# Attention values with a 37-column stationary operand, and its accumulator read by VectorE in two parts

## The chip, the cores and the metric

The kernel runs on one core of one Trainium2 chip. The metric is the device time of one execution in microseconds, the median of the runs shown. Lower is better. The engines are called TensorE (PE in the profile, PEld for its weight loads), VectorE (DVE), ScalarE (ACT), GpSimd (POOL) and SyncE (SP, which issues transfers).

## The reference

One block of a conditioned transformer, all in fp32: x is 2 x 2048 x 576, 16 heads of 36 features, a hidden layer of 2304.

```python
mod = silu(c) @ w_ada + b_ada                      # six vectors per batch: shifts, scales, gates
xn = layernorm(x) * (1 + sc_msa) + sh_msa
q, k, v = split(xn @ w_qkv + b_qkv)                # 16 heads of 36
q, k = layernorm(q, qn_g, qn_b), layernorm(k, kn_g, kn_b)
attn = softmax(einsum('bqhd,bkhd->bhqk', q, k) * 36 ** -0.5)
o = einsum('bhqk,bkhd->bqhd', attn, v)
x = x + g_msa * (o @ w_proj + b_proj)
xn2 = layernorm(x) * (1 + sc_mlp) + sh_mlp
x = x + g_mlp * (gelu(xn2 @ w1 + b1) @ w2 + b2)
```

## The kernel before

Each of the two batches goes through its queries, keys and values, then attention (`attend`, called once per batch), then the projection of the output; the hidden layer for both batches comes last. The change is in `attend`.

Attention works on pairs of heads (8), blocks of 512 queries (4) and groups of 4 x 128 keys (4): 128 steps per batch. A step has three parts.

- `scores` (L1536) makes scores transposed, with keys on partitions. Each of its two half steps fills four PSUM banks of 128 x 512, one for each of the four groups of 32 rows of TensorE's array, which work side by side. A bank gets two products: 32 of a head's 36 features (`qm`, `km`), then the other 4 in three parts (`qe`, `ke`). ScalarE takes the exponential of each bank (L1540) into a tile `pt` in SBUF, of which there are five.
- `values` (L1549) multiplies the step's eight exponentials with the values and adds them up in one bank, the accumulator: head 0 of the pair in its rows 0 to 63, head 1 in rows 64 to 127. The stationary operand is 64 columns of `vt` from the head's first one. A head has 37 columns there (`HV`): its 36 values and a column of ones, whose product is the softmax's denominator. The other 27 columns belong to the next head; the rows of the accumulator that they make are not used.
- VectorE reads the accumulator, all 128 rows at once, into an SBUF tile `ot`: copied in the first key group (L1603), added in the other three (L1605).

After the fourth group `finish` sends the two rows of denominators (row 36 of either half) to DRAM and back on 64 partitions each, and VectorE divides: a reciprocal of `den` (L1570) and a product over all 128 rows of `ot` (L1571). These are put into a list of later work and come some steps behind.

The eight banks of PSUM are one ring (`bank()`, a pool of eight buffers). A step takes nine: eight for scores and one for the accumulator. TensorE's and VectorE's instructions stand in the order in which the code is written. The loop issues the scores of a step first, and then the values of the step before it. The accumulator's bank comes up again eight banks later, as the last of the eight that the next step's scores fill: the fourth of its second half.

Two steps of the loop carry other work in hooks (L178 is the product of the conditioning weights). For the last accumulator of a batch `ot` is the spare tile `spare[9]`.

Of the kernel before, what the change touches and what calls it, by code (L numbers as in the profile page):

```python
# [8 lines left out]
F32 = mybir.dt.float32  # L9
# [3 lines left out]
ALU = mybir.AluOpType  # L13
# [3 lines left out]
P = 128  # L17
# [14 lines left out]
def dit_block(  # L32
# [25 lines left out]
    nc = tc.nc  # L58
# [7 lines left out]
    BLK = 512  # L66
    NBLK = N // BLK
    TPB = BLK // P
    NF = MLP // P
    HV = HD + 1  # L70
# [23 lines left out]
    def bank():  # L94

        return psum["b"].tile([P, 512], F32, tag="b", name="b") if "b" in psum else s_tile()[:, 0, :]
# [650 lines left out]
    def head_rows(first, count=HD):  # L747

        at = first
        while at < first + count:  # L750
            n = min(P - at % P, first + count - at)
            yield at // P, at % P, at - first, n
            at += n

    def block_of_small():
# [11 lines left out]
        held, spare = {}, []  # L767
# [10 lines left out]
        vt = kv.tile([P, NT * H * HV + 64 - HV], F32, name="vt")  # L778
# [85 lines left out]
        def take_k(p):  # L864
            m, e = km[p % 2], ke[p % 2]
            if p > 2:
                not_sooner(m)
                not_sooner(e)
            src = lambda c: slice(c * N // 2, (c + 1) * N // 2)
            rows_taken(nc.gpsimd, m, e, range(2), C + p * 2 * HD, src, slice(0, N // 2))  # L870
            full = slice(0, P)
            return [
                lambda: scaled(m, m, full, 1),
                lambda: parted(e[:, 0:BLK], full, 1),
                lambda: parted(e[:, BLK:], full, 1),
            ]
# [13 lines left out]
        def take_q(p, qb):  # L890
            i, full = qb % 2, slice(0, P)
            src = lambda c: slice(qb * BLK, (qb + 1) * BLK)
            rows_taken(nc.sync, qm[i], qe[i], range(2), p * 2 * HD, src, slice(0, BLK))
            return [lambda: scaled(qm[i], qm[i], full, 0), lambda: parted(qe[i], full, 0)]
# [623 lines left out]
        def attend(b, pool, hooks, key_rows):  # L1518

            def scores(p, qb, g):
                i, j = p % 2, qb % 2
                pts = []
                for k0 in (2 * g * P, (2 * g + 1) * P):
                    keys = slice(k0, k0 + P)
                    banks = [bank() for _ in range(4)]
                    for k, q, first in (  # L1530
                        (km[i], qm[j], True),
                        (ke[i].bitcast(F32R), qe[j].bitcast(F32R), False),
                    ):
                        for r0, ps in zip(range(0, P, 32), banks):
                            r = slice(r0, r0 + (DIMS if first else 4 * (HD - DIMS)))
                            nc.tensor.matmul(ps, k[r, keys], q[r, :], start=first, stop=not first)  # L1536
                    for c in range(2):
                        pt = pool.tile([P, 2, BLK], F32, name="pt", bufs=5)
                        for h in range(2):
                            nc.scalar.activation(pt[:, h, :], banks[2 * c + h], AF.Exp, scale=SCALE)  # L1540
                        pts.append((pt, k0 // P + c * NT // 2))
                return pts

            def values(p, pts):
                acc = bank()
                for pt, kc in pts:
                    for h in range(2):
                        v0 = (kc * H + 2 * p + h) * HV
                        nc.tensor.matmul(  # L1549
                            acc[64 * h : 64 * h + 64, :],  # L1550
                            vt[:, v0 : v0 + 64],
                            pt[:, h, :],
                            start=pt is pts[0][0],
                            stop=pt is pts[-1][0],
                        )
                return acc

            def finish(p, qb, ot, den=None):


                if den is None:
                    den = pool.tile([P, BLK], F32, name="den")
                for h in range(2):
                    sums = den_dram[b, p, qb, h, :]
                    nc.sync.dma_start(out=sums.unsqueeze(0), in_=ot[64 * h + HD : 64 * h + HD + 1, :])
                    nc.sync.dma_start(out=den[64 * h : 64 * h + 64, :], in_=sums.partition_broadcast(64))

                def divided(c0=0, c1=BLK):
                    part = slice(c0, c1)
                    nc.vector.reciprocal(den[:, part], den[:, part])  # L1570
                    nc.vector.tensor_tensor(ot[:, part], ot[:, part], den[:, part], ALU.mult)  # L1571
                    cols = slice(qb * BLK + c0, qb * BLK + c1)
                    for h in range(2):
                        for c, row, d, n in head_rows((2 * p + h) * HD):
                            for r in (row,) if c < FULL else (row, row + 64):
                                nc.sync.dma_start(
                                    out=held["qo"][r : r + n, c, cols], in_=ot[64 * h + d : 64 * h + d + n, part]
                                )

                return divided  # L1580

            steps = [(p, qb, g) for p in range(NPAIR) for qb in range(NBLK) for g in range(NG)]


            behind, later = None, [[] for _ in range(13)]
            ended = None
            for p, qb, g in [*steps, (None, None, None)]:
                pts = None if p is None else scores(p, qb, g)
                if (p, qb) == (0, 0) and g < len(key_rows):
                    key_rows[g]()  # L1590
                if g == 0 and (p, qb) != (NPAIR - 1, NBLK - 1):
                    for i, do in enumerate(take_q(*((p, qb + 1) if qb + 1 < NBLK else (p + 1, 0)))):
                        later[1 + i].append(do)
                if g == 1 and qb == 0 and p + 1 < NPAIR:
                    for i, do in enumerate(take_k(p + 1)):
                        later[3 + NG * i].append(do)
                if behind is not None:
                    bp, bqb, bg, bpts = behind
                    acc = values(bp, bpts)
                    if bg == 0:  # L1600
                        last = (bp, bqb) == (NPAIR - 1, NBLK - 1)
                        ot = spare[9][:, :BLK] if last else pool.tile([P, BLK], F32, name="ot", bufs=2)
                        nc.vector.tensor_copy(ot, acc)  # L1603
                    else:
                        nc.vector.tensor_tensor(ot, acc, ot, ALU.add)  # L1605
                    if p is None:
                        ended = finish(bp, bqb, ot, spare[10][:, :BLK])
                    elif bg == NG - 1:
                        later[2 if bp == NPAIR - 1 else 3].append(finish(bp, bqb, ot))
                if (p, qb, g) in hooks:  # L1610
                    due = hooks[p, qb, g]() or []
                    later[1] = due[:1] + later[1]
                    later[2] = due[1:] + later[2]
                later.append([])
                for do in later.pop(0):
                    do()
                behind = (p, qb, g, pts)
            for do in [do for group in later for do in group]:
                do()
            return ended  # L1620
# [411 lines left out]
        for j in range(TPB + 1):  # L2032
            n, i = divmod(j, TPB)
# [346 lines left out]
        def combined_blocks(out_m, outs):  # L2380

            one = hs.tile([P, QUARTER], F32, name="one", bufs=2)
            nc.scalar.copy(one, out_m[1])  # L2383
            r = hs.tile([P, 2, HALF], F32, name="r", bufs=9)
            left, right = r[:, :, 0:QUARTER], r[:, :, QUARTER:HALF]
            both = lambda ap: ap.unsqueeze(1).to_broadcast([P, 2, QUARTER])
            tt = nc.vector.tensor_tensor
            tt(left, outs[2, 6], both(one), ALU.add)
            tt(right, outs[5, 7], both(left[:, 1]), ALU.add)
            tt(left[:, 1], right[:, 1], out_m[4], ALU.subtract)  # L2390
            tt(right[:, 1], right[:, 1], out_m[5], ALU.add)
            tt(right[:, 0], right[:, 0], out_m[3], ALU.add)
            return r
# [57 lines left out]
        for i, (n, m) in enumerate(products):  # L2451
# [16 lines left out]
            r = combined_blocks(out_m, outs)  # L2468
# [67 lines left out]
```

## Time and profile before

| what | us |
|---|---|
| median of 3 runs | 3060.53 (3060.13 to 3061.5) |
| span of the profiled execution | 3061.8 |
| TensorE busy in it | 3039.6 |
| VectorE busy | 1706.3 |
| ScalarE busy | 1493.3 |
| GpSimd busy | 1000.6 |
| products of the values, L1549 | 935.0 busy, 4096 |
| reads of the accumulator into `ot`, L1603 and L1605 | 42.9 and 128.6 busy, 62 and 186 |

The profiled execution has no other time of its own than its span, from the first to the last instruction. The granted TensorE clock was 0.999 in it. An fp32 product shows as two records, so the 4096 records of L1549 are 2048 products. A row of a timeline gives the start in us from the span's start, the length in us, the engine and line, the operation, the tile written and those read, and how many records are merged; in brackets, for how long the engine had been idle and what ended that. A row of the groups gives busy time and mean ns of one, then the idle time ahead of it. A row of one line's instructions gives shortest, middle and longest ns.

### The profile page before, as it was taken

To read this page: it belongs to the slowest core of one execution; us is meant where nothing else is said; L and a number is where in the kernel's file an instruction comes from. 1 tells how busy PE (TensorE), PEld (TensorE's weight loads), DVE (VectorE), ACT (ScalarE), POOL (GpSimd) and SP (SyncE) were. 2 spreads that over 40 slices of the span, in tenths; PEclk is the share of its full clock that TensorE was granted. 3 is DMA by queue.
4 is the path that set the end of the run, shared out by engine and by line. 5 is a ranking of instruction groups with operands and counts; after the bars stand their busy time and mean duration, and the time that the engine had idled before them with its cause. 6 is when DMAs were issued, how large, how long until landed. Compare 5 with 4: busy or idle time off the path is not lost.

```text
span 3061.8 us, 51356 instructions
## 1 busy us (share of the span) xinstructions
PE 3039.6 (99%) x19015; PEld 1892.7 (62%) x19015; DVE 1706.3 (56%) x2644; ACT 1493.3 (49%) x2917; POOL 1000.6 (33%) x1263
## 2 busy tenths in 40 slices
PE   8999999999999999999999999999999999999998
PEld 6884333333333688633333333347888888999998
DVE  6773455445553666544434444447666664667666
ACT  2326666666666233466666666643555553000000
POOL 4551100132322445201101111115445544545543
PEclk9999999999999999999999999999999999999999
DMA  5773322333333454412222222236888887855554
GB/s 150 187 147 92 103 69 70 81 92 93 94 87 94 162 129 83 94 46 64 52 55 74 62 67 66 77 97 191 250 239 241 243 243 290 311 190 198 206 188 150
DMA packets 427940, 415.17 MB, mean 136 GB/s; under 512 B 231473, under 2 KB 355921, under 8 KB 419553
## 3 DMA queue, kind: packets, MB, share of 16 engines
q1 hardware_dynamic: 390520, 314.46, 34.4%
q0 software_dynamic: 36848, 97.33, 11.7%
q8 instruction: 153, 2.51, 0.3%
q14 instruction: 107, 0.87, 0.1%
q10 hardware_dynamic: 312, 0.01, 0.0%
HBM read 246.43 MB, written 154.75 MB: 131 GB/s over the span
## 4 chain that ended last, share of the span: by engine, by line
PE 99%; DVE 0%; ACT 0%; issue 0%; POOL 0%; DVEq 0%
PE b L1549 30%; PE b L1536 20%; PE b L2366 12%; PE m L2107 12%; PE s L1141 7%; PE s L1227 5%; PE s L1717 4%; PE m L2121 2%; PE one L2107 2%; PE b L2375 2%; PE s L1143 1%; PE s L1233 1%; PE s L1714 1%; PE b L178 0%; PE s L1229 0%; ACT xnt L398 0%
## 5 line engine op out<-in xcount | busy, mean ns | idle before, releaser
L1540 ACT ACTIVATE pt<-b 128x512 f32<-128x512 f32 x2048 | 1057.2, 610 | 482.6 <-PE b L1549 269.4
L1549 PE MATMUL b<-pt,vt 128*64 128x512 f32 x4096 | 935.0, 599 | 0.0
L1549 PEld LDWEIGHTS b<-pt,vt 128*64 128x64 f32 x4096 | 271.9, 136 | 582.0 <-issue 437.6
L1536 PE MATMUL b<-qm,km 32*128 32x512 f32 x4096 | 563.8, 613 | 0.0
L1605 DVE TENSOR_TENSOR ot<-b,ot 128x512 f32<-128x512 f32 x186 | 128.6, 691 | 546.4 <-PE b L1549 546.4
L1536 PE MATMUL b<-qe,ke 16*128 16x512 f32 x2048 | 420.4, 791 | 0.0
L1536 PEld LDWEIGHTS b<-qm,km 32*128 32x128 f32 x4096 | 190.8, 185 | 270.9 <-ACT pt L1540 211.1
L1141 PE MATMUL s<-wq,xnt 128*128 128x288 f32 x864 | 226.7, 406 | 1.5 <-ACT xnt L398 1.5
L2383 ACT COPY one<-b 128x144 f32<-128x144 f32 x55 | 15.3, 278 | 406.0 <-PE b L2366 406.0
L2107 PE MATMUL m<-xnt,wb 128*128 128x256 f32 x864 | 209.1, 379 | 1.4 <-issue 1.3
L2107 PE MATMUL m<-s,wb 128*128 128x256 f32 x864 | 207.4, 379 | 0.0
L1570 DVE RECIPROCAL den<-den 128x512 f32<-128x512 f32 x62 | 206.8, 3336 | 0.0
L1603 DVE COPY ot<-b 128x512 f32<-128x512 f32 x62 | 42.9, 691 | 259.1 <-PE b L1549 253.8
L1141 PEld LDWEIGHTS s<-wq,xnt 128*128 128x128 f32 x864 | 158.0, 190 | 36.9 <-ACT xnt L398 2.2
L1536 PEld LDWEIGHTS b<-qe,ke 16*128 16x128 f32 x2048 | 107.0, 184 | 113.6 <-issue 112.8
L2107 PEld LDWEIGHTS m<-s,wb 128*128 128x128 f32 x864 | 163.6, 190 | 22.0
L2107 PEld LDWEIGHTS m<-xnt,wb 128*128 128x128 f32 x864 | 159.4, 190 | 21.5 <-issue 1.7
L2145 ACT ACTIVATE cs<-cs,b_sb 128x512 f32<-128x512 f32 x144 | 100.1, 720 | 137.8 <-DVE cs L2140 137.6
L1802 POOL DMA_DIRECT2D spare<-in_x_dram x32 | 17.8, 556 | 451.5 <-DVE met L794 451.5
L2147 POOL TENSOR_TENSOR cs<-cs 128x256 f32<-128x256 f32 x72 | 57.5, 798 | 244.5 <-ACT cs L2145 244.5
L1062 ACT ACTIVATE xnt<-xnt,mod 128x128 f32<-128x128 f32 x244 | 100.1, 482 | 51.1 <-DMA xnt<-turned 51.1
L2134 DVE TENSOR_TENSOR cs<-m,cs 128x512 f32<-128x512 f32 x72 | 49.3, 684 | 118.9 <-PE m L2121 76.0
(374 smaller groups left out, 4590.3 us busy)
## 6 DMA issues: line engine op xcount, KB each, us to landing
operands<-cs SPq DMA_DIRECT2D x70, 896.0 KB
wb<-operands SPq DMA_DIRECT2D x37, 1152.0 KB
operand<-operands SPq DMA_DIRECT2D x19, 1152.0 KB
spare<-in_x_dram POOLq DMA_DIRECT2D x64, 288.0 KB, 3.2
x_dram<-spare POOLq DMA_DIRECT2D x64, 288.0 KB, 2.4
qm<-qk SPq DMA_DIRECT2D x256, 64.0 KB
den<-den_dram SPq DMA_DIRECT2D x124, 128.0 KB
spare<-x_dram POOLq DMA_DIRECT2D x37, 288.0 KB, 3.9
```

Source lines behind the costliest of these rows:

```text
L1062: nc.scalar.activation(part, part, AF.Identity, **affine(which, k, b))
L1141: nc.tensor.matmul(out_a, full[:, k, :], wq[:, k, f], start=k == 0, stop=False)
L1227: nc.tensor.matmul(out[m], x_[:, k, :], w_(k), start=k == 0, stop=k == 1 and m == 6)
L1536: nc.tensor.matmul(ps, k[r, keys], q[r, :], start=first, stop=not first)
L1540: nc.scalar.activation(pt[:, h, :], banks[2 * c + h], AF.Exp, scale=SCALE)
L1549: nc.tensor.matmul(acc[64 * h : 64 * h + 64, :], vt[:, v0 : v0 + 64], pt[:, h, :], start=pt is pts[0][0], stop=pt is pts[-1][0],)
L1570: nc.vector.reciprocal(den[:, part], den[:, part])
L1605: nc.vector.tensor_tensor(ot, acc, ot, ALU.add)
L1717: nc.tensor.matmul(out[m], x_[m][:, k], factors[m][:, k], start=k == 0 and m not in (3, 4), stop=k == 1 and m not in (2, 7),)
L2107: nc.tensor.matmul(out_m[m], wb[:, f, slot[m], k, :], moving[m](k), start=k == 0 and m in firsts, stop=k == 1 and m in lasts,)
L2145: nc.scalar.activation(part, part, AF.Gelu, bias=b1_sb[:, g : g + 1])
L2366: nc.tensor.matmul(out_m[m], stationary[m][:, c, :], w[:, 7 * c + m - 1, :], start=a == 0 and c == 0, stop=ends and c == FULL - 1 and m no ...
```

## The change

The stationary operand of the values has the head's own 37 columns, so the accumulator gets rows 0 to 36 and 64 to 100. VectorE reads it in two instructions, rows 0 to 36 and then rows 64 to 100, each into the same rows of `ot`. The two tiles that `ot` turns between are taken once, ahead of the loop, and GpSimd fills their rows 32 to 63 and 96 to 127 with ones, since `finish` multiplies all 128 rows.

```diff
@@ values @@
                         nc.tensor.matmul(
-                            acc[64 * h : 64 * h + 64, :],
-                            vt[:, v0 : v0 + 64],
+                            acc[64 * h : 64 * h + HV, :],
+                            vt[:, v0 : v0 + HV],
                             pt[:, h, :],
@@ attend, ahead of the loop @@
             behind, later = None, [[] for _ in range(13)]
+            ots = [pool.tile([P, BLK], F32, name=f"ot{i}") for i in range(2)]
+            for at in ots:
+                for r0 in (32, 96):
+                    nc.gpsimd.memset(at[r0 : r0 + 32, :], 1.0)
@@ attend, in the loop @@
                     acc = values(bp, bpts)
                     if bg == 0:
                         last = (bp, bqb) == (NPAIR - 1, NBLK - 1)
-                        ot = spare[9][:, :BLK] if last else pool.tile([P, BLK], F32, name="ot", bufs=2)
-                        nc.vector.tensor_copy(ot, acc)
-                    else:
-                        nc.vector.tensor_tensor(ot, acc, ot, ALU.add)
+                        ot = spare[9][:, :BLK] if last else ots[(bp * NBLK + bqb) % 2]
+                    for r in (slice(64 * h, 64 * h + HV) for h in range(2)):
+                        if bg == 0:
+                            nc.vector.tensor_copy(ot[r], acc[r])
+                        else:
+                            nc.vector.tensor_tensor(ot[r], acc[r], ot[r], ALU.add)
```

The diff moves the lines behind it by four to six: the copy is L1609 and the addition L1611 in the changed kernel.

TensorE in the middle of attention, one step and the half step behind it (`b` is a bank; a name ending in `_49` is an engine's or a queue's semaphore). Before:

```order
L1536 MATMUL b<-qm_217,km_216 128x512 [waits Activation_49] x4
L1536 MATMUL b<-qe_220,ke_218 128x512 x4
L1536 MATMUL b<-qm_217,km_216 128x512 [waits Activation_49] x3
L1536 MATMUL b<-qm_217,km_216 128x512 [waits DVE_49]
L1536 MATMUL b<-qe_220,ke_218 128x512 x4
L1549 MATMUL b<-pt,vt 64x512 [waits Activation_49]
L1549 MATMUL b<-pt,vt 64x512 x7
```

With the change:

```order
L1536 MATMUL b<-qm_217,km_216 128x512 [waits Activation_49] x4
L1536 MATMUL b<-qe_220,ke_218 128x512 x4
L1536 MATMUL b<-qm_217,km_216 128x512 [waits Activation_49] x3
L1536 MATMUL b<-qm_217,km_216 128x512 [waits DVE_49]
L1536 MATMUL b<-qe_220,ke_218 128x512 x4
L1549 MATMUL b<-pt,vt 37x512 [waits Activation_49]
L1549 MATMUL b<-pt,vt 37x512 x7
```

Order and waits are the same; the values' products have 37 columns. In both, the fourth product of the second half step waits for VectorE.

VectorE around a division (`den` are the denominators, `ot` the sums; L850 to L860 prepare the next keys). Before:

```order
L1605 TENSOR_TENSOR ot<-b,ot 128x512 [waits PE_49]
L1570 RECIPROCAL den<-den 128x512 [waits DMAHW2_49,DMAHW1_49]
L1571 TENSOR_TENSOR ot<-ot,den 128x512 [waits DMAHW7_49,DMAHW0_49,DVE_49]
L1605 TENSOR_TENSOR ot<-b,ot 128x512 [waits PE_49]
L794 COPY met<-spare 1x1 [waits Pool_49]
```

With the change:

```order
L1611 TENSOR_TENSOR ot_1822<-b,ot_1822 37x512 [waits PE_49]
L1611 TENSOR_TENSOR ot_1822<-b,ot_1822 37x512
L1570 RECIPROCAL den<-den 128x512 [waits DMAHW2_49,DMAHW1_49]
L1571 TENSOR_TENSOR ot_1823<-ot_1823,den 128x512 [waits DMAHW7_49,DMAHW0_49,DVE_49]
L1611 TENSOR_TENSOR ot_1822<-b,ot_1822 37x512 [waits PE_49]
L1611 TENSOR_TENSOR ot_1822<-b,ot_1822 37x512
L794 COPY met<-spare 1x1 [waits Pool_49]
```

Where one read stood now stand two, back to back; the first waits for TensorE, the second for nothing. On GpSimd the four fills stand at the start of either batch's attention, directly ahead of the loads of the second pair's keys (L815, L817).

## The prediction

> **What bounds the kernel now.** I read the page's engine table and its chain of waits first, then the costliest groups, then the timeline of one step of attention, and last a step that went otherwise than its neighbours.
>
> ```profile
> span 3061.8 us, 51356 instructions
> ...
> PE 3039.6 (99%) x19015; PEld 1892.7 (62%) x19015; DVE 1706.3 (56%) x2644; ACT 1493.3 (49%) x2917; POOL 1000.6 (33%) x1263
> ...
> PE 99%; DVE 0%; ACT 0%; issue 0%; POOL 0%; DVEq 0%
> PE b L1549 30%; PE b L1536 20%; PE b L2366 12%; PE m L2107 12%; PE s L1141 7%; PE s L1227 5%; PE s L1717 4%; PE m L2121 2%; PE one L2107 2%; PE b L2375 2%; PE s L1143 1%; PE s L1233 1%; PE s L1714 1%; PE b L178 0%; PE s L1229 0%; ACT xnt L398 0%
> ...
> L1549 PE MATMUL b<-pt,vt 128*64 128x512 f32 x4096 | 935.0, 599 | 0.0
> L1605 DVE TENSOR_TENSOR ot<-b,ot 128x512 f32<-128x512 f32 x186 | 128.6, 691 | 546.4 <-PE b L1549 546.4
> L1603 DVE COPY ot<-b 128x512 f32<-128x512 f32 x62 | 42.9, 691 | 259.1 <-PE b L1549 253.8
> ```
>
> TensorE is the bound, and half of the chain is attention: values (L1549) and scores (L1536). VectorE looks free: 56% busy, waiting for TensorE before its reads of the accumulator. But a share over the span does not say when a bank has to be free. One step does:
>
> ```profile
> 500.36 3.65 PE L1549 MATMUL b<-pt,vt 128*64 128x512 f32 x16
> 503.95 1.14 PE L1536 MATMUL b<-qm,km 32*128 32x512 f32 x8
> 504.06 0.69 DVE L1605 TENSOR_TENSOR ot<-b,ot 128x512 f32<-128x512 f32 x1 [2.49 <-PE b L1549]
> 504.91 0.44 PEld L1536 LDWEIGHTS b<-qm,km 32*128 32x128 f32 x8 [0.22 <-issue]
> 505.15 1.03 PE L1536 MATMUL b<-qm,km 32*128 32x512 f32 x8
> 505.61 0.81 PE L1536 MATMUL b<-qe,ke 16*128 16x512 f32 x4
> 506.35 3.65 PE L1549 MATMUL b<-pt,vt 128*64 128x512 f32 x16
> ```
>
> A step lasts 506.35 - 500.36 = 5.99 us: values, then two half steps of scores (503.95 and 505.15). VectorE reads the accumulator from 504.06 to 504.75. The weights of the second half start loading at 504.91. By the order of the program the fourth product of that half goes into the bank that VectorE has just read: its ring has eight banks, a step takes nine, so the accumulator's comes round as the last of the next eight. So VectorE has until shortly after 504.75, not until the next accumulator 6 us later.
>
> How long exactly is seen where VectorE was late by chance, behind a division:
>
> ```profile
> 955.10 3.65 PE L1549 MATMUL b<-pt,vt 128*64 128x512 f32 x16
> ...
> 958.58 0.69 DVE L1571 TENSOR_TENSOR ot<-ot,den 128x512 f32<-128x512 f32 x1
> ...
> 959.19 0.69 DVE L1605 TENSOR_TENSOR ot<-b,ot 128x512 f32<-128x512 f32 x1
> ...
> 959.65 0.57 PEld L1536 LDWEIGHTS b<-qm,km 32*128 32x128 f32 x8 [0.22 <-issue]
> 959.88 1.03 PE L1536 MATMUL b<-qm,km 32*128 32x512 f32 x7
> ...
> 960.46 0.59 PE L1536 MATMUL b<-qm,km 32*128 32x512 f32 x1
> ...
> 961.21 3.65 PE L1549 MATMUL b<-pt,vt 128*64 128x512 f32 x16
> ```
>
> Here the read began 959.19 - 955.10 = 4.09 us after its values instead of 504.06 - 500.36 = 3.70: late by 0.39. The eight weight loads of the second half spread over 0.57 us instead of 0.44, one product fell behind the others (960.46), and the step lasted 961.21 - 955.10 = 6.11 us, 0.12 longer. So of a delay of the accumulator's release **the first 0.27 us are free, and the rest is paid in full by TensorE**. This step is the scale for what follows.
>
> **The change part by part.**
>
> *Two reads instead of one.* Each read covers 37 partitions and still 512 elements per partition. Whether fewer partitions make it shorter is told by these rows of VectorE, as is how closely two such instructions follow each other:
>
> ```profile
> 785.36 0.69 DVE L1605 TENSOR_TENSOR ot<-b,ot 128x512 f32<-128x512 f32 x1 [3.57 <-PE b L1549]
> 785.97 0.44 DVE L1644 TENSOR_TENSOR wp<-wp,gate 64x288 f32<-64x288 f32 x1
> 786.44 0.45 DVE L1645 TENSOR_TENSOR wp<-wp,gate 64x288 f32<-64x288 f32 x1
> 786.93 0.45 DVE L1646 TENSOR_TENSOR wp_less<-wp_less,gate 64x288 f32<-64x288 f32 x1
> ...
> 1018.69 0.46 DVE L1752 TENSOR_TENSOR vt<-vt,s 128x288 f32<-128x288 f32 x1 [0.94 <-PE s L1717]
> ```
>
> 64 partitions by 288 took 0.44 to 0.45 us, 128 by 288 took 0.46: the number of partitions does not shorten it. Each half read is therefore taken at 0.69. Spacing: L1644 started 0.61 us after the 0.69 us instruction ahead of it, 0.08 before that one's end. Both start at partition 0. L1645 works on partitions 64 to 127 behind L1644 on 0 to 63, depends on nothing of it, and started 0.47 after a 0.44 us instruction: 0.03 after its end. The way back (L1646, from partition 0 again) costs the same. The second read is just such a pair, 0 then 64. So it should start 0.69 + 0.03 = 0.72 us after the first and end 0.72 later than the single read ends now. The nearest rows bound this: 0.61 if it overlaps like L1644, 0.72 if it goes like L1645. I take 0.72, since the partitions are those of L1645.
>
> The Trainium skill, "VectorE: DVE Perf Modes", section "Two Vector instructions with no wait between them", gives a model in which an instruction is held until all earlier Vector instructions have finished when an operand starts in another group of 32 partitions than the last one in that memory; the rows above agree (0.03 after the end against 0.08 before it). By the rule the step pays 0.45 us, without it 0.34.
>
> Price per step: 0.72 - 0.27 = 0.45 us on TensorE. What hides the rest is the 0.27 just measured, and nothing else does: queued behind the waiting product on TensorE are the small products of all four row groups and then the values, which need the whole array. How many steps: 248 accumulators in the two groups above, and 8 more that go into a spare tile, are 256. The last two of each batch have no scores after them, and in one step of each batch 3 us of another product stands between values and scores:
>
> ```profile
> 344.37 3.65 PE L1549 MATMUL b<-pt,vt 128*64 128x512 f32 x16
> 347.96 3.03 PE L178 MATMUL b<-wa,sil 128*32 128x320 f32 x40
> 350.92 1.14 PE L1536 MATMUL b<-qm,km 32*128 32x512 f32 x8
> ...
> 510.05 0.69 DVE L1605 TENSOR_TENSOR ot<-b,ot 128x512 f32<-128x512 f32 x1 [1.31 <-PE b L1549]
> ```
>
> That leaves 250, so **250 x 0.45 = 112.5 us**. VectorE itself keeps up: it has 0.72 more to do in a step that is 0.45 longer, so its idle time shrinks by 0.27, and behind a division, its longest piece, 1.31 was idle (510.05). Only in steps like that at 955.10, of which I count four, it is already late; there the lateness grows by the same 0.27 + 0.72, some 0.54 more than elsewhere: 4 x 0.54 = 2.2 us.
>
> *37 columns instead of 64.* Products stream the same 512 columns. What could get shorter is the load of the weights, where it is not hidden:
>
> ```profile
> L1549 PE MATMUL b<-pt,vt x4096: 592/592/645, 242.6 to 2040.9; 128*64 128x512 f32 x196
> ...
> L1536 PE MATMUL b<-qm,km x4096: 585/587/692, 235.9 to 2033.7; 32*128 32x512 f32 x196
> ...
> 506.83 0.14 PEld L1549 LDWEIGHTS b<-pt,vt 128*64 128x64 f32 x2 [0.28 <-issue]
> 507.26 0.14 PEld L1549 LDWEIGHTS b<-pt,vt 128*64 128x64 f32 x2 [0.28 <-issue]
> ```
>
> The middle of L1549's products is 592 ns, equal to the shortest, the longest 645: only the first pair of a step contains its load, some 53 ns. With 128 columns (L1536) the longest exceeds the middle by 105. That is 0.8 ns per column, so 27 columns fewer save 22 ns per step: 256 x 0.022 = **5.6 us gained**. Within the step loads come 0.43 us apart and take 0.14, under the products of the pair ahead. Bounds: nothing gained, or all eight pairs shortened, 45 us; the middle of 592 speaks for the first pair alone.
>
> The Trainium skill, "TensorE: Matmul & The Clock Gate", section "Part 3: Packing small matmuls — row/col tiling", says that a load overlaps a product in flight only when its row group differs; here all loads use all rows, so each would be exposed. The rows differ from it: 592 is both shortest and middle. What it would give is a rival below.
>
> *The fill of the two output tiles*, four on GpSimd per batch, and the end of the second batch:
>
> ```profile
> L787 POOL MEMSET qe<- 128x512 f32 x2 | 1.0, 542 | 0.0
> ...
> 246.35 0.69 DVE L1603 COPY ot<-b 128x512 f32<-128x512 f32 x1 [5.88 <-PE b L1549]
> ...
> 2041.59 0.69 DVE L1605 TENSOR_TENSOR spare<-b,spare 128x512 f32<-128x512 f32 x1 [2.77 <-PE b L1549]
> ...
> 2042.34 2.21 PE L1717 MATMUL s<-wp,qo 128*128 128x288 f32 x8 [0.82 <-DVE spare L1605]
> ```
>
> Four fills at 0.54 us are 2.2 us on GpSimd, ahead of its loads of the second pair's keys, which nothing needs for some steps, and in time for the first copy at 246.35, provided the transfers that they wait for have landed. Bounds 0 to 2 us; I take 0. At the end of the second batch TensorE waits for the last read: 0.72 once more.
>
> **Sum**: 112.5 + 2.2 + 0.7 - 5.6 = +109.8 us on the span of 3061.8, so 3171.6. The runs' median, 3060.53, is 1.3 below that span; 3060.5 + 109.8 = 3170.3, in round numbers **3171 us**, 3.6% slower.
>
> **The rivals.**
>
> *The second read overlaps the first* (as L1644 does): 0.61 - 0.27 = 0.34 per step, 27.5 us less: 3143. Against it stands L1645.
>
> *The release never decides* and the kernel gets faster: each half read ends soon enough for both to fit into 0.69 + 0.27 us, or the other three row groups take up the delay, and only the loads' 5.6 us count: 3055. For it: VectorE's 546 us of idle. Against it: both reads would have to take no more than 0.46 us each, and the step at 955.10 shows that nothing takes up a delay beyond 0.27. From that point it is lost.
>
> *Every load counts*: 45 instead of 5.6 us gained, 3131.
>
> *VectorE falls behind in more steps*, those with a division: 62 of them, each up to the 0.54 of the late steps, 33 us: 3204. Against: the 1.31 idle at 510.05.
>
> *The heads lose their column halves* and no longer run side by side: sixteen products at 0.43 one after another instead of eight pairs add 3.44 us per step, 256 x 3.44 = 880: some 4050. The second head still begins at row 64, which speaks against it, but no row shows a 37-column operand.
>
> **How the numbers follow.** Forecast 82%; overlap 8%; every load 3%; more steps late 4%; never decides 2%; halves lost 1%. The forecast's own range follows from the unknowns on either side: free time 0.25 to 0.29, the gap 0.02 to 0.05, the loads 0 to 5.6, the fills 0 to 2: about 3158 to 3187. The 8 in 10 range takes in part of the overlap case: **3150 to 3188**. A difference of 0.2%, 6 us, is about what a measurement of this kernel can tell from no change. All cases but one lie far above: slower 0.96, same 0.02, faster 0.02.
>
> **What would show it.** A regular step of 6.44 us. Behind each first read a second at 0.72, with the same 0.69. In the waits, the weight loads of L1536 waiting for VectorE's read in about 250 places, where now there is almost none. In the chain, VectorE with about 250 x 1.4 us, 11%, where now 0% stands. The longest L1549 product near 622 ns instead of 645, the middle unchanged. The forecast is wrong if the second read starts before the first ends, if steps stay at 5.99, or if the loss is unevenly spread over the steps.

## The result, and the profile after

| | before | after |
|---|---|---|
| median of 5 runs, us | 3060.53 (3060.13 to 3062.17) | 3176.28 (3174.26 to 3176.43) |
| span of the profiled execution, us | 3061.8 | 3174.5 |

The ratio is 1.0373, 95% interval 1.036 to 1.0385: 110 to 118 us slower. The forecast was 3171 (3150 to 3188).

From the page of the changed kernel: the span, TensorE's busy time, the chain by engine and by line, and four groups.

```profile
span 3174.5 us, 51683 instructions
...
PE 3151.8 (99%) x19015; PEld 1908.1 (60%) x19015; DVE 1904.5 (60%) x2900; ACT 1493.6 (47%) x2917; POOL 1004.5 (32%) x1271
...
PE 98%; DVE 1%; DMA 0%; issue 0%; ACT 0%; SPq 0%; POOL 0%; DVEq 0%
PE b L1549 28%; PE b L1536 23%; PE b L2372 12%; PE m L2113 12%; PE s L1141 7%; PE s L1227 4%; PE s L1723 4%; PE m L2127 2%; PE one L2113 2%; PE b L2381 2%; PE s L1143 1%; PE s L1233 1%; PE s L1720 1%; DVE den L1570 0%; DMA wa<-in_w_ada_dram 0%; DVE ot L1611 0%
...
L1549 PE MATMUL b<-pt,vt 128*37 128x512 f32 x4096 | 929.3, 596 | 0.0
L1536 PE MATMUL b<-qm,km 32*128 32x512 f32 x4096 | 682.0, 620 | 1.0 <-DVE ot L1611 1.0
...
L1611 DVE TENSOR_TENSOR ot<-b,ot 37x512 f32<-37x512 f32 x372 | 256.1, 688 | 485.2 <-PE b L1549 479.9
...
L1609 DVE COPY ot<-b 37x512 f32<-37x512 f32 x124 | 85.4, 688 | 237.7 <-PE b L1549 235.8
```

The row of the scores in the page of before:

```profile
L1536 PE MATMUL b<-qm,km 32*128 32x512 f32 x4096 | 563.8, 613 | 0.0
```

A reader who looks at TensorE's share alone sees nothing: 99% busy before and after. But its busy time grew by 112 us for the same products. The scores' busy time went from 563.8 to 682.0 though one product takes hardly longer (613 and 620 ns), and their share of the chain from 20% to 23%. A group's busy time is far below its count times its mean (4096 x 0.613 = 2511), so it is the time in which at least one of its records runs: what ran side by side now runs one behind the other. One step of the changed kernel, in order of time, shows it:

```profile
510.69 3.63 PE L1549 MATMUL b<-pt,vt 128*37 128x512 f32 x16
...
514.26 1.14 PE L1536 MATMUL b<-qm,km 32*128 32x512 f32 x8
514.38 1.39 DVE L1611 TENSOR_TENSOR ot<-b,ot 37x512 f32<-37x512 f32 x2 [3.45 <-PE b L1549]
...
515.22 0.44 PEld L1536 LDWEIGHTS b<-qm,km 32*128 32x128 f32 x6 [0.22 <-issue]
515.46 1.06 PE L1536 MATMUL b<-qm,km 32*128 32x512 f32 x7
...
515.82 0.18 PEld L1536 LDWEIGHTS b<-qm,km 32*128 32x128 f32 x1 [0.16 <-DVE ot L1611]
...
515.92 0.80 PE L1536 MATMUL b<-qe,ke 16*128 16x512 f32 x3
...
516.36 0.59 PE L1536 MATMUL b<-qm,km 32*128 32x512 f32 x1
...
516.38 0.80 PE L1536 MATMUL b<-qe,ke 16*128 16x512 f32 x1
...
517.11 1.48 PE L1549 MATMUL b<-pt,vt 128*37 128x512 f32 x5
```

The step lasts 517.11 - 510.69 = 6.42 us instead of 5.99. VectorE's two reads begin at the old place, 3.69 behind the values, and take 1.39 together instead of 0.69. They end at 515.77, and 0.05 later, at 515.82, the fourth product's weights start to load. Its second pass runs from 516.36. The last products of the other three row groups began at 515.92 and end at 516.72; the fourth group's began only at 516.38, and the values start behind it, at 517.11.

For the whole of line 1536 (what its engines waited for: us, times), and for the products and weight loads of line 1549 (shortest, middle, longest ns):

```profile
  DVE ot L1611: 37.3, 187
  DVE ot L1609: 11.6, 62
```

```profile
L1549 PEld LDWEIGHTS b<-pt,vt x4096: 109/114/115, 241.5 to 2153.0; 128*37 128x37 f32 x196
L1549 PE MATMUL b<-pt,vt x4096: 592/592/622, 241.5 to 2153.4; 128*37 128x512 f32 x196
```

These are 187 + 62 = 249 waits for VectorE's reads into `ot`. Four of the 187 are products of the late steps shown next and not loads; four more loads wait for the reads into the spare tile, so 249 loads wait as well, one a step. The longest product of the values fell from 645 to 622 ns, the middle stayed at 592.

The step where VectorE is late behind a division went like this (the first two rows from VectorE's own timeline, the others from that of all engines):

```profile
1002.32 1.41 DVE L1611 TENSOR_TENSOR ot<-b,ot 37x512 f32<-37x512 f32 x2 [3.16 <-PE b L1549]
1003.76 0.55 DVE L850 TENSOR_SCALAR ended<-qe,gb_at 128x512 f32<-128x512 f32 x1
...
1005.53 3.34 DVE L1570 RECIPROCAL den<-den 128x512 f32<-128x512 f32 x1
```

```profile
1005.06 3.63 PE L1549 MATMUL b<-pt,vt 128*37 128x512 f32 x16
...
1008.91 0.69 DVE L1571 TENSOR_TENSOR ot<-ot,den 128x512 f32<-128x512 f32 x1
...
1009.63 1.41 DVE L1611 TENSOR_TENSOR ot<-b,ot 37x512 f32<-37x512 f32 x2
...
1011.10 0.18 PEld L1536 LDWEIGHTS b<-qm,km 32*128 32x128 f32 x1 [1.08 <-DVE ot L1611]
...
1012.38 1.06 PE L1549 MATMUL b<-pt,vt 128*37 128x512 f32 x4
```

It lasts 1012.38 - 1005.06 = 7.32 us, 1.21 more than the 6.11 before. There are four such steps in either kernel.

The middle step of the trace is 6.425 us, before it was 5.984 (values' first product to the next step's, 249 steps that have nothing else in between; the 250th has a small other product). Of these 250 steps, 246 x 0.441 = 108.5 and 4 x 1.21 = 4.8 make 113.3, against 112.7 us between the spans: the loss is in these steps, spread evenly over all but the four late ones.

### The profile page after: what moved, and what is told of

Same layout as the page of the kernel before. It is cut to its first block, busy times and chain, and to the rows that moved or that the text cites. A ratio compares the mean times of both kernels' runs of the same rounds, so it can differ in the third digit from the quotient of the medians.

```text
span 3174.5 us, 51683 instructions
## 1 busy us (share of the span) xinstructions
PE 3151.8 (99%) x19015; PEld 1908.1 (60%) x19015; DVE 1904.5 (60%) x2900; ACT 1493.6 (47%) x2917; POOL 1004.5 (32%) x1271
## 4 chain that ended last, share of the span: by engine, by line
PE 98%; DVE 1%; DMA 0%; issue 0%; ACT 0%; SPq 0%; POOL 0%; DVEq 0%
PE b L1549 28%; PE b L1536 23%; PE b L2372 12%; PE m L2113 12%; PE s L1141 7%; PE s L1227 4%; PE s L1723 4%; PE m L2127 2%; PE one L2113 2%; PE b L2381 2%; PE s L1143 1%; PE s L1233 1%; PE s L1720 1%; DVE den L1570 0%; DMA wa<-in_w_ada_dram 0%; DVE ot L1611 0%
## 5 line engine op out<-in xcount | busy, mean ns | idle before, releaser
L1549 PE MATMUL b<-pt,vt 128*37 128x512 f32 x4096 | 929.3, 596 | 0.0
L1536 PE MATMUL b<-qm,km 32*128 32x512 f32 x4096 | 682.0, 620 | 1.0 <-DVE ot L1611 1.0
L1549 PEld LDWEIGHTS b<-pt,vt 128*37 128x37 f32 x4096 | 224.5, 114 | 617.7 <-issue 475.6
L1611 DVE TENSOR_TENSOR ot<-b,ot 37x512 f32<-37x512 f32 x372 | 256.1, 688 | 485.2 <-PE b L1549 479.9
L1536 PE MATMUL b<-qe,ke 16*128 16x512 f32 x2048 | 535.5, 789 | 0.0
L1536 PEld LDWEIGHTS b<-qm,km 32*128 32x128 f32 x4096 | 259.6, 184 | 327.2 <-ACT pt L1540 215.9
L1609 DVE COPY ot<-b 37x512 f32<-37x512 f32 x124 | 85.4, 688 | 237.7 <-PE b L1549 235.8
L1536 PEld LDWEIGHTS b<-qe,ke 16*128 16x128 f32 x2048 | 150.3, 184 | 119.3 <-issue 118.3
L1570 DVE RECIPROCAL den<-den 128x512 f32<-128x512 f32 x62 | 207.1, 3340 | 0.8
```

The costliest lines, as they stand in the source:

```text
L1549: nc.tensor.matmul(acc[64 * h : 64 * h + HV, :], vt[:, v0 : v0 + HV], pt[:, h, :], start=pt is pts[0][0], stop=pt is pts[-1][0],)
L1611: nc.vector.tensor_tensor(ot[r], acc[r], ot[r], ALU.add)
```

## The experiments

The theory has two halves: TensorE waits for the *end of the last read of the bank*, and the second read ends late because it *begins at another partition*. The rivals are that VectorE simply has more to do, and that any second instruction costs as much. The scale (0.27 us free, the rest in full) and the price of the columns were measured as well. All runs are timed beside the kernel before on the same chip; its median was 3061.54 there for the first four and 3061.34 for the others.

### The same work behind the read

```diff
+        twice = ended
...
                         nc.vector.tensor_tensor(ot, acc, ot, ALU.add)
+                    at = slice(64, 64 + HV)
+                    nc.vector.tensor_tensor(twice[at], ot[at], ot[at], ALU.add)
```

`ended` is a scratch tile in SBUF.

> The kernel before with one more VectorE instruction of the same 0.69 us per accumulator, but behind the whole read and on SBUF only. The bank is released when it was. If the release decides, steps stay at 5.99 us and only the four steps in which VectorE is already late pay up to 0.8 us each: 3060.5 + 3 = 3064 us. If VectorE's amount of work decides, the time is that of the change, about 3175 us.

Measured: 3065.9 us (3064.04 to 3067.75), ratio 1.0014 (1.0004 to 1.0023). A step in its timeline:

```profile
506.94 3.65 PE L1550 MATMUL b<-pt,vt 128*64 128x512 f32 x16
...
510.64 0.69 DVE L1606 TENSOR_TENSOR ot<-b,ot 128x512 f32<-128x512 f32 x1 [0.46 <-PE b L1550]
...
511.36 0.69 DVE L1608 TENSOR_TENSOR ended<-ot 37x512 f32<-37x512 f32 x1
...
512.93 3.65 PE L1550 MATMUL b<-pt,vt 128*64 128x512 f32 x16
```

The extra instruction has the second read's length (0.69) and its place (0.72 behind the first), but doesn't touch the bank. The step stays at 5.99. So the amount of work is not the cause. The middle step is 5.985 against 5.984. What remains, 4.4 us between the medians, lies in a few steps: the four late ones behind a division last 6.95 to 6.97 instead of 6.10 to 6.11, 3.4 us together, about as expected, and two others are longer by 0.34 and 0.44.

### An extra read ahead, from row 0 and from row 64

```diff
+        twice = ended
...
                     acc = values(bp, bpts)
+                    nc.vector.tensor_copy(twice[0:HV], acc[0:HV])
```

and the same with `64 : 64 + HV` on both sides; behind it the whole bank is read as before.

> The kernel before with one more read, rows 0 to 36 of the accumulator into an idle tile, ahead of the whole read. Both begin at partition 0. If an instruction that begins at the same partition as the last may overlap it, the whole read begins 0.61 us after the extra one, the step pays 0.61 - 0.265 = 0.345 us, and the time is 3060.5 + 250 x 0.345 + 3 = 3150 us. If any second read of the bank waits for the end of the first, 0.72 and 3060.5 + 250 x 0.455 + 3 = 3177 us.

> As the run with the extra read from row 0, but the extra read takes rows 64 to 100; the whole read behind it begins at partition 0. If a change of the first partition makes the next instruction wait for the end of the last, 0.72 between the starts, 0.455 us per step and 3177 us. If it does not, 0.61 and 3150 us, as in the other run.

Measured: 3164.31 (3163.28 to 3166.9), ratio 1.0334 (1.0319 to 1.035) from row 0; 3199.12 (3198.32 to 3199.54), ratio 1.045 (1.0434 to 1.0466) from row 64. The two reads in the timeline of the first, then of the second kernel:

```profile
514.85 0.68 DVE L1601 COPY ended<-b 37x512 f32<-37x512 f32 x1 [3.66 <-PE b L1550]
...
515.46 0.67 DVE L1607 TENSOR_TENSOR ot<-b,ot 128x512 f32<-128x512 f32 x1
```

```profile
517.64 0.69 DVE L1601 COPY ended<-b 37x512 f32<-37x512 f32 x1 [3.66 <-PE b L1550]
...
518.35 0.69 DVE L1607 TENSOR_TENSOR ot<-b,ot 128x512 f32<-128x512 f32 x1
```

Two instructions that both begin at row 0 follow each other at 0.61, 0.07 before the first one's end; from row 64 to row 0 it is 0.71, behind the end. Nothing but the rows differs, and the runs are 34.8 us apart, 0.14 a step. So the change of the first partition is the cause of the spacing: this is shown, not only argued from L1645.

Both runs missed what was expected, by 14 and 22 us on the slow side, so something else costs more as well. The next pair found it.

### 64 columns, and rows read or not

The change's two reads with the old columns, against the changed kernel:

```diff
-                            acc[64 * h : 64 * h + HV, :],
-                            vt[:, v0 : v0 + HV],
+                            acc[64 * h : 64 * h + 64, :],
+                            vt[:, v0 : v0 + 64],
```

> Two reads as in the change, but the stationary operand has 64 columns again. If the loss is the second read's alone, the step is 6.45 us (the change's 6.425 plus the 0.022 us of a longer exposed load), the longest product of L1549 is back at 645 ns, and the time is 3176 + 5.6 = 3182 us. If the 37-column operand has a cost of its own on TensorE, the time falls below 3176; if all of the loss were its own, to 3060.

Measured: 3197.25 (3196.29 to 3197.73), ratio 1.0443 (1.0429 to 1.0457): 15 us more than expected. One line and one step of this kernel (its waits on TensorE that are instructions of their own, then the reads and the fourth product's weights):

```profile
L1536 PEldq EVENT_SEMAPHORE  x629: 51/51/3492, 231.2 to 2167.2; - x158
```

```profile
511.66 1.41 DVE L1609 COPY ot<-b 37x512 f32<-37x512 f32 x2 [3.08 <-PE b L1549]
...
513.18 0.18 PEld L1536 LDWEIGHTS b<-qm,km 32*128 32x128 f32 x1 [0.24 <-PE b L1536]
```

In the changed kernel line 1536 has 377 such waits, here 629, some 250 more: one a step. In the list of TensorE's instructions the fourth product waits here for VectorE and for TensorE's own semaphore, there for VectorE alone: 27 rows of either half were written and are left out by the reads, and I took it that the bank's next writer therefore has to wait for their writer too. The weights start 513.18 - 513.07 = 0.11 us behind the read instead of 0.05. If that is the cause, it goes away when all 64 rows of either half are read:

```diff
-                    for r in (slice(64 * h, 64 * h + HV) for h in range(2)):
+                    for r in (slice(64 * h, 64 * h + 64) for h in range(2)):
```

> 64 columns and two reads as in e2, but each read takes all 64 rows that its head's products write, so that TensorE's fourth product waits for VectorE alone, as in the change; in e2 it also waited for a semaphore of TensorE's own, and its weight load began 0.116 us behind VectorE's end instead of 0.053. If that second wait is why e2 was 21 us above the change and not 5.6, the time is 3182 us (step 6.447). If 37 columns are worth 21 us to TensorE, it is 3197 us as in e2 (step 6.51).

Measured: 3182.22 (3181.25 to 3183.03), ratio 1.0392 (1.0378 to 1.0407), as expected.

```profile
L1536 PEldq EVENT_SEMAPHORE  x377: 51/51/3496, 230.7 to 2128.8; - x189
```

```profile
515.34 1.39 DVE L1611 TENSOR_TENSOR ot<-b,ot 64x512 f32<-64x512 f32 x2 [3.48 <-PE b L1549]
...
516.78 0.18 PEld L1536 LDWEIGHTS b<-qm,km 32*128 32x128 f32 x1 [0.16 <-DVE ot L1611]
```

So 15 us of the miss was a second wait that has long been met when its turn comes, and still takes a 51 ns instruction behind VectorE's release. The two kernels with an extra read have it too. And 37 columns instead of 64 are worth 3182.22 - 3176.28 = 5.9 us; the middle steps, 6.449 and 6.425, say the same.

That rows which nobody reads bring the second wait is not borne out by the other runs, though. The run of the next section leaves a whole half unread and doesn't have it, while two reads by columns (below) take in every row and have it. Their rows, in this order:

```profile
L1536 PEldq EVENT_SEMAPHORE  x377: 51/51/3460, 232.5 to 2007.8; - x189
```

```profile
L1536 PEldq EVENT_SEMAPHORE  x629: 51/51/3492, 231.8 to 2033.4; - x158
```

In all eleven kernels of this document the second wait stands where some read takes only a part of the rows or columns that one product has written, and in no other; no run was made to test this rule by itself.

### Half of the reading

```diff
-                for r0 in (32, 96):
+                for r0 in (32, 64, 96):
...
-                    for r in (slice(64 * h, 64 * h + HV) for h in range(2)):
+                    for r in (slice(64 * h, 64 * h + HV) for h in range(1)):
```

The changed kernel without its second read: the sums of each pair's second head are left out, and their rows of the tile are filled once.

> The change with only the first of the two reads: the sums of each pair's second head are left out. The 37-column operand stays, and the bank is released when it was before. If the 37 columns are worth the exposed part of one pair of loads, 0.022 us per step, the step is 5.963 us and the time 3061 - 5.6 = 3055 us, about 0.2% faster. If they are worth 21 us, 3040 us; if nothing, 3061 us.

Measured: 3054.78 (3054.32 to 3057.16), ratio 0.9978 (0.9969 to 0.9987).

```profile
505.92 3.63 PE L1549 MATMUL b<-pt,vt 128*37 128x512 f32 x16
...
509.60 0.68 DVE L1611 TENSOR_TENSOR ot<-b,ot 37x512 f32<-37x512 f32 x1 [1.30 <-PE b L1549]
...
510.44 0.44 PEld L1536 LDWEIGHTS b<-qm,km 32*128 32x128 f32 x8 [0.22 <-issue]
...
511.88 3.63 PE L1549 MATMUL b<-pt,vt 128*37 128x512 f32 x16
```

A step of 5.96, with the eight loads in 0.44 again. The whole loss hangs on the second read, and without it the columns give 6.6 us, close to the 5.9 above. 37 rows took 0.68 us, 128 take 0.69.

### The scale: a little late, and more than a little

Two reads of 256 columns each, all rows:

```diff
-                        nc.vector.tensor_copy(ot, acc)
-                    else:
-                        nc.vector.tensor_tensor(ot, acc, ot, ALU.add)
+                    for c in (slice(0, BLK // 2), slice(BLK // 2, BLK)):
+                        if bg == 0:
+                            nc.vector.tensor_copy(ot[:, c], acc[:, c])
+                        else:
+                            nc.vector.tensor_tensor(ot[:, c], acc[:, c], ot[:, c], ALU.add)
```

> The kernel before with the read cut by columns: all 128 rows by 256 columns, twice, both from partition 0. Two reads as in the change, but the second ends only some 0.07 us later than the single one did; the fourth product has the second wait of 0.06 us. Together 0.13 us, below the 0.27 us that are free: steps stay at 5.99 us and the time at 3062 us. If a second read costs something by being one, the time is above 3080 us.

Measured: 3062.56 (3060.7 to 3067.54), ratio 1.0004 (0.9994 to 1.0013).

The extra read from row 0 with 320 columns only:

```diff
+        twice = ended
...
                     acc = values(bp, bpts)
+                    nc.vector.tensor_copy(twice[0:HV, 0:320], acc[0:HV, 0:320])
```

> The kernel before with an extra read of rows 0 to 36 by 320 columns ahead of the whole read. The whole read begins some 0.41 us later. With the second wait on the fourth product (0.06 us) 0.47 us late, of which 0.27 are free: 0.20 us per step, 50 us, 3113 us. If the second wait costs nothing, 0.14 us per step and 3098 us. If the loss has no free part, 0.41 us per step and 3165 us.

Measured: 3114.66 (3113.55 to 3115.57), ratio 1.0171 (1.0155 to 1.0187). The reads of the former, then of the latter, in their timelines:

```profile
509.97 0.76 DVE L1607 TENSOR_TENSOR ot<-b,ot 128x256 f32<-128x256 f32 x2 [1.24 <-PE b L1549]
```

```profile
511.25 0.48 DVE L1601 COPY ended<-b 37x320 f32<-37x320 f32 x1 [2.30 <-PE b L1550]
511.66 0.67 DVE L1607 TENSOR_TENSOR ot<-b,ot 128x512 f32<-128x512 f32 x1
```

Two instructions from the same row cost 0.76 - 0.69 = 0.07 together, which is free. With 320 columns the reads end at 512.33, 1.08 behind their start instead of 0.69, 0.39 late, and this is past the free time.

All steps on one scale. Each number is the middle one of 249 steps, from the start of the values' first product. Worked out: how late the last read ends, less 0.254, and 0.063 more where the fourth product has the second wait.

| kernel | last read ends, us | late | second wait | step longer, worked out | measured |
|---|---|---|---|---|---|
| before | 4.393 | | no | | (step 5.984) |
| work behind the read | 4.393 | 0 | no | 0 | 0.001 |
| two reads by columns | 4.459 | 0.066 | yes | 0 | -0.003 |
| extra read, 320 columns | 4.783 | 0.390 | yes | 0.199 | 0.201 |
| extra read from row 0 | 4.982 | 0.589 | yes | 0.398 | 0.403 |
| extra read from row 64 | 5.119 | 0.726 | yes | 0.535 | 0.536 |
| 64 columns, 37 rows read | 5.111 | 0.718 | yes | 0.527 | 0.527 |
| 64 columns, 64 rows read | 5.112 | 0.719 | no | 0.465 | 0.465 |
| the change | 5.087 | 0.694 | no | 0.440 | 0.441 |

0.254 is from the one kernel that has 64 columns and one wait, and 0.063 from the pair that differs in the wait; the other rows are tests of them. They fit within 5 ns. The change's reads end 0.025 sooner than the same reads with 64 columns, since its first pair of values is 0.023 shorter (622 against 645 ns): that is where the columns' gain enters.

### Columns without the second read

What is left of the idea is a single read with fewer columns. With 37 columns in both heads one read would take in rows of the bank that no product of that accumulator has written, so this was not tried. Head 0 with 64 columns and head 1 with 37, read together as rows 0 to 100, is possible:

```diff
-                            acc[64 * h : 64 * h + 64, :],
-                            vt[:, v0 : v0 + 64],
+                            acc[64 * h : 64 * h + (64, HV)[h], :],
+                            vt[:, v0 : v0 + (64, HV)[h]],
...
+            r = slice(0, 64 + HV)
...
-                        nc.vector.tensor_copy(ot, acc)
+                        nc.vector.tensor_copy(ot[r], acc[r])
...
-                        nc.vector.tensor_tensor(ot, acc, ot, ALU.add)
+                        nc.vector.tensor_tensor(ot[r], acc[r], ot[r], ALU.add)
```

> Head 0 keeps its 64 columns, head 1 has 37, and VectorE reads rows 0 to 100 in one instruction. One read that starts at row 0 ends 0.69 us after its start, as before, so no step gets longer on VectorE's account. What is left is the load of the first pair. If both heads' loads are exposed, about half of the 22 ns a step is gained: 250 x 0.011 = 2.8 us, 3058. If the longer load sets the pair, nothing: 3061. If the last load sets it, all of it: 3055. None of the theories has it above the kernel before by more than its own spread.

Measured: 3060.29 (3059.39 to 3063.82), ratio 0.9998 (0.9989 to 1.0007). Its row of the values' products:

```profile
L1549 PE MATMUL b<-pt,vt x4096: 592/592/644, 242.8 to 2039.4; 128*64 128x512 f32 x99, 128*37 128x512 f32 x97
```

The longest product is as long as before, and the step is 5.977, 7 ns shorter: 2 us at most, which the runs don't tell from nothing.

## Why the prediction was right, and where it was off

- **What bounds.** That the release of the accumulator's bank, and not VectorE's load, decides: right. Moving the same work behind the read took the loss away, and so did leaving out the second read. The rivals in which the release never decides and in which the heads lose their halves are gone with it (products of one pair still run side by side: the sixteen records of a step take 3.63 us).
- **The second read at 0.72, 0.69 long**: right, 0.714 in the middle and 0.69. The overlap rival is settled by the pair of extra reads: two that start at row 0 overlap, one from row 64 and one from row 0 do not. The Trainium skill, "VectorE: DVE Perf Modes", section "Two Vector instructions with no wait between them", names the quarter of the partitions where an operand starts as what holds an instruction; the pair (0.61 against 0.71, only the rows changed) agrees.
- **0.27 us free**: a little too much. It is 0.254, which over 250 steps is 4 us, more than the 2.9 that the sum lacked; against it stands the second read at 0.714 instead of 0.72, 1.5 us. It was read from one step whose rows are rounded to 0.01 us.
- **The late steps**: this term was wrong by its reasoning. I let them grow by 0.27 + 0.72 = 0.99 us; they grew by 1.21. In the rows of that step the query's scaling (L850) starts 0.03 behind the second read's end, where before it started 0.08 before the end (952.82 + 0.69 and 953.43), and L1611 starts 0.03 behind L1571's end, where before it started 0.08 before it. Two more places of 0.11 each that I left out: in both, the way back to row 0 is held like the way to row 64. The second is remarkable, as L1570 and L1571 lie in between and begin at partition 0. But they don't touch PSUM, and by the section just named the last start is kept for SBUF and PSUM apart; that fits. The run with the same work behind the read tells it: there an instruction at rows 64 stands in the same place but reads SBUF alone, and the read of the bank behind the same product (L1572 there) is not held. It starts 0.61 behind it, in all four late steps, where in the changed kernel it is 0.72:

```profile
960.01 0.69 DVE L1572 TENSOR_TENSOR ot<-ot,den 128x512 f32<-128x512 f32 x1
960.62 0.68 DVE L1606 TENSOR_TENSOR ot<-b,ot 128x512 f32<-128x512 f32 x1
```

Two places in four steps make it 0.9 us.
- **The end of the second batch**, 0.7: right. In the list of who waited for L1611, TensorE's next product stands with 1.5 us, where before it was 0.82:

```profile
  PE s L1723: 1.5, 1
```

- **5.6 us for the shorter loads**: right. 5.9 us between two kernels that differ in the columns and in the rows read with them, 6.6 in the one with one read. "Every load counts", 45 us, is out: the middle product did not get shorter. That is where the Trainium skill, "TensorE: Matmul & The Clock Gate", section "Part 3: Packing small matmuls — row/col tiling", which in its list lets a load overlap only a product in another row group, differs from what was measured: all these loads use all rows and only a step's first pair shows one.
- **GpSimd's fills at nothing**: right. They took 0.52 us each, and nothing waited for them:

```profile
L1589 POOL MEMSET ot<- x8: 516/518/562, 234.7 to 1329.6; 32x512 f32 x8
```

- **More late steps**: no; four, as before.
- **The count of 250 steps**: right, but I had one detail wrong. The two steps with the product L178 both lie in the first batch (344.37 and 443.09 in the trace of before), none in the second.
- **The sum**: +109.8 worked out, +112.7 between the spans. The medians are 115.7 apart. The other 3 us are those by which before's profiled execution was slower than its median: a run takes 1.9 us more than its span (3176.43 and 3174.5 in the profiled run after), so that execution took about 3063.7. I had added the difference to the median, as if it stood where the span does. The low end of the range doesn't follow from its unknowns: 250 x (0.69 + 0.02 - 0.29) = 105, with 2.2 + 0.7 - 5.6 some 102, so about 3163 and not 3158.
- **What would show it**: a step of 6.44 (it is 6.425) and 250 waiting loads (249) came. VectorE with 11% of the chain did not: 1%. The chain follows an engine's own work as long as it is busy, and TensorE's other three row groups were busy while the fourth product waited. The waiting loads were idle for only 0.16 to 0.2 us of the 0.44. The loss appears as a larger share of L1536 instead. This was an error about the view, not about the kernel.

## What to carry to other kernels

Before an instruction that frees a buffer is split, work out from one step by when the buffer's next writer needs it: the delay up to then is the whole budget, however idle the engine looks over the span. The gap in a regular step is only a first guess: from the read's end to the first load of the half step it was 0.16 us here, and 0.254 were free. A step that was late by chance told it better. Two VectorE reads are nearly free against one when they start at the same partition and split the columns (0.07 us here), and cost the full second length when they split the partitions, because an instruction of 512 elements took 0.68 to 0.69 us here whether it covered 37, 64 or 128 of them. Let every read take all that a product has written, or the bank's next user may get one more wait; this is the pattern of the runs here, not a rule that was tested.

## What the runs showed that was not expected

- A wait on TensorE that is already met is not free when it comes on top of another: as the product waits for two semaphores, one of the waits becomes an instruction of 51 ns, and the weight load starts 0.116 instead of 0.053 us behind the release. Over 250 steps that was 15 us. In the kernel with two reads by columns the same waits cost nothing, since the release is not late there.
- After a step of VectorE to another partition and back, the next instruction is held as well, 0.11 us each time; only the four late steps had no slack to hide it.
- TensorE's busy share stayed at 99% while it lost 113 us. What fell was how many products ran side by side, and a group's busy time against its count and mean tells it (563.8 to 682.0 us at 613 and 620 ns).
